# Order of the second conv's statistics and copy, aggregates by chunk, and first units in halves in a two-layer convolution kernel

## Chip, cores and metric

The kernel runs on one core of one Trainium2 chip. The metric is device time in microseconds (us) for one execution. TensorE is called PE here, VectorE DVE, ScalarE ACT, GpSimd POOL, and SyncE SP; SP issues nearly all DMAs. Each of these engines takes its instructions in order from a queue of its own.

## What is computed

The input is x, four images of 128 channels and 128 x 128 pixels, in fp32. Layer 0 is region attention (16 x 16 regions with a step of 14, four heads), merged back into an image `xf`, then a projection to 256 channels, a depthwise 5 x 5 convolution, a batch norm over all images, two Gelus, a projection back, and a residual. Layer 1 is two quantised 3 x 3 convolutions with batch norms. Cut to what matters here:

```python
y  = ln(xf) @ w_p0 + b_p0                  # 256 channels
ym = depthwise_5x5(y)
ym = batchnorm(ym)                         # mean and variance over images and pixels
y  = gelu(gelu(ym)) @ w_p2 + b_p2 + xf     # = x of layer 1, kept as identity

q   = round(clip(y, 0, 1) * 15)            # act_quant
c1  = conv3x3(q, quantised(w1))
q2  = round(clip(batchnorm(c1), 0, 1) * 15)
c2  = conv3x3(q2, quantised(w2))
out = batchnorm(c2) + identity
```

Each batch norm needs all of its input before the first output: three points at which all images must be through.

## The kernel before

Channels lie on the 128 partitions. The work has four stages.

**Attention and depthwise convolution** (to about 2316 us). Attention goes by bands of regions; the depthwise convolution runs beside it, and for its last unit (the last quarter of the last image) after it, in `conv_rest`. `conv_rest` goes through eight chunks k of 32 channels. Each `step(k)` does 256 and more small matmuls (L590), two ACT copies out of PSUM (L710), eight `bn_stats` on DVE (L714) and stores to DRAM (L719). The statistics lie in `st0`.

**Aggregation** (L1059 to L1079, then `affine`, L999 to L1005). 64 `bn_aggr` turn `st0` into `mvp` (one mean and variance for each of 64 groups); squares are added; the four channels that share a row are spread apart by products with `quad` (L1069, eight instructions into `ex`); four matmuls (L1071) sum over partitions; `affine` makes scale and shift for the Gelu. This part is not under a hand-written order: the planner places its instructions.

**Gelu stage** (`gelu_stage`). 64 units of 8 rows (U = 1024 pixels), 16 for each image. For each unit n: load `cv` (1 MB, L1185) and `xf` (512 KB, L1190) from DRAM, two Gelus (`gelus`: L1196 twice for the two channel halves with scale and shift, L1199 over both), the second projection (eight PE matmul instructions, L1208), bias and residual on DVE (L1216, writes y), clip on POOL (L1220), two quantising steps on DVE (L1226 and `to_int`, L1162) into the padded image `q1[b]`, and, two units behind, the first 3 x 3 convolution (`conv3x3`, 18 matmuls, L1150), its statistics (`stats_of`, L1158) and a copy out (`keep`, L1232). y is stored to `id_d` and the convolution to `c1_d`; the last image's convolution stays on chip in `c1_s`. The three buffers `cv` and `xfl` each are handed on from unit to unit.

**Last stages** (`last_stages`). A first pass over all 64 units: load `c1` (images 0 to 2 only, three buffers; for image 3 it is `c1_s`), relu with scale and shift on ACT (L1302), two quantising steps on DVE (L1303, L1162) into `q1[b]`, and behind it the second convolution with its statistics; for image 3, the 16 late units, ACT also copies the convolution out to `c1_s` (L1310). Then batch norm 2 (`rest2`) and a second pass, in which the convolution of images 0 to 2 is computed again and scaled (L1319), the identity added (L1320) and the result stored.

`most1` and `most2` aggregate the statistics of the first 120 of 128 half units ahead of time (L1025); `rest1` and `rest2` aggregate what is left and make scale and shift (L1034 to L1041).

The conv work, the Gelu stage and the last stages stand in `tc.manual_schedule(engines=MANUAL)`: PE, ACT, DVE and SP run in the order in which the code emits, POOL does not. So the order of the lines in the loop below is the order of each queue:

```python
for n in range(len(units) + 2):
    ...load_first(n + 2), load_id...
    if n < len(units):
        relu (ACT) of n; min/round (DVE) of n; to_int (DVE) of n
    if n >= 2:
        conv3x3 (PE) of n - 2; stats_of (DVE) of n - 2; copy (ACT) of n - 2 if image 3
```

PSUM tiles `pc` of the last stages have four buffers of two banks. A conv of unit n reads rows of units n-1, n and n+1 of `q1`.

Of the kernel before, what the change touches and what calls it, by code (L numbers as in the profile page):

```python
# [14 lines left out]
P = 128  # L15
# [31 lines left out]
def layers(  # L47
# [49 lines left out]
    c1_d = [dram.tile([P, P * P], F32, name=f"c1_d{b}") for b in range(B - 1)]  # L97
    id_d = [dram.tile([P, P * P], F32, name=f"id_d{b}") for b in range(B)]

    def vector(v, name):  # L100
        n = v.shape[0] // P
        t = const.tile([P, n], F32, name=name)
        nc.sync.dma_start(out=t, in_=v.rearrange("(h p) -> p h", p=P))
        return t

# [27 lines left out]
    with (  # L133
# [33 lines left out]
    units = [(b, 0, P // GR) for b in range(B - 1)] + [(B - 1, g, n) for g, n in ((0, 4), (4, 2), (6, 2))]  # L167

    sctx = ctx.enter_context(ExitStack())
    st0 = sctx.enter_context(tc.tile_pool(name=f"st0_{tag}", bufs=1)).tile(  # L170
        [P, NCK, 2, 4, len(units), 6], F32, name="st0"
    )


    with ExitStack() as actx:
# [492 lines left out]
        def conv_rest(n, w_t, u_t, c_t):  # L668

            b, g0, ng = units[n]
            early = 3
            at = GR + 2

            def load(k, a, z, g, m):
                for half in range(2):
                    ch = 32 * k + 16 * half
                    nc.sync.dma_start(
                        out=U[k][64 * half + 2 * a : 64 * half + 2 * z, g : g + m].rearrange(  # L680
                            "p g c x -> p g (c x)"
                        ),
                        in_=input_of(b, g0 + g, m, ch, 16, a, z),
                    )

            U = [u_t.tile([P, ng, 16, CW], F32, name=f"u{k}") for k in range(NCK)]
            W = [w_t.tile([P, 3, 16, 32], F32, name=f"w{k}") for k in range(NCK)]
            for k in range(NCK):
                weights(W[k], k, 0, 2, nc.gpsimd.dma_start)
            for k in range(early):  # L690
                load(k, 0, at, 0, 1)

            def late(k):
                if k < early:
                    load(k, 0, at, 1, 1)
                    load(k, at, GR + 4, 0, ng)
                else:
                    load(k, 0, GR, 0, ng)
                    load(k, GR, GR + 4, 0, ng)

            def step(k):
                sc = ps_s.tile([P, 2, 2, NT], F32, name=f"sc{k % 2}")
                pc = [
                    sc[:, half].rearrange("p a n -> p (a n)").rearrange("p (j g x) -> p j g x", j=4, g=ng)
                    for half in range(2)
                ]
                depthwise(pc, W[k], U[k], 16)
                for half in range(2):
                    cv = c_t.tile([P, 4, ng, CW], F32, name=f"c{half}")
                    nc.scalar.copy(  # L710
                        cv.rearrange("p j g x -> p (j g x)"), pc[half].rearrange("p j g x -> p (j g x)")
                    )
                    for j in range(4):
                        nc.vector.bn_stats(  # L714
                            st0[:, k, half, j, n, :], cv[:, j].rearrange("p g x -> p (g x)")
                        )
                    engine = (nc.sync, nc.scalar)[half]
                    for g in range(ng):
                        engine.dma_start(  # L719
                            out=bass.AP(  # L720
                                cv_d[b].tensor,
                                cv_d[b][g0 + g, 32 * k + 16 * half, 0:1].offset,
                                [[CW, P], [4 * GR * P, 4], [1, CW]],
                            ),
                            in_=cv[:, :, g],
                        )

            def run_all():
                for k in range(4):
                    late(k)  # L730
                for k in range(NCK):
                    step(k)
                    if k + 4 < NCK:
                        late(k + 4)

            return run_all
# [312 lines left out]

    mv0 = const.tile([P, 2, 2], F32, name="mv0")  # L1050
    with (
        tc.tile_pool(name=f"bn0_{tag}", bufs=1) as bn0,
        tc.tile_pool(name=f"ps_q_{tag}", bufs=1, space=PSUM) as ps_q,
    ):
        nk = NCK * 2 * 4
        mv = bn0.tile([P, 2, nk], F32, name="mvp")
        flat = st0.rearrange("p k a j n s -> p (k a j) (n s)")
        for k in range(nk):
            nc.vector.bn_aggr(mv[:, :, k], flat[:, k, :])  # L1059
        sq = bn0.tile([P, nk], F32, name="sqp")  # L1060
        nc.vector.tensor_tensor(sq, mv[:, 0, :], mv[:, 0, :], ALU.mult)
        nc.vector.tensor_tensor(mv[:, 1, :], mv[:, 1, :], sq, ALU.add)
        all1 = bn0.tile([P, 1], F32, name="all1")
        nc.vector.memset(all1, 1.0 / 32)
        pq = ps_q.tile([P, 2, 2], F32, name="pq")
        for m in range(2):
            ex = bn0.tile([P, nk, 4], F32, name=f"ex{m}")
            for q in range(4):
                nc.vector.tensor_scalar(ex[:, :, q], mv[:, m, :], quad[:, q : q + 1], None, ALU.mult)  # L1069
            for h in range(2):  # L1070
                nc.tensor.matmul(  # L1071
                    pq[:, m, h : h + 1],
                    ex.rearrange("p k q -> p (k q)")[:, h * P : (h + 1) * P], all1,
                    start=True, stop=True,
                )
        nc.vector.tensor_copy(mv0, pq)
        sq0 = bn0.tile([P, 2], F32, name="sq0")
        nc.vector.tensor_tensor(sq0, mv0[:, 0, :], mv0[:, 0, :], ALU.mult)
        nc.vector.tensor_tensor(mv0[:, 1, :], mv0[:, 1, :], sq0, ALU.subtract)  # L1079
    sc0, sh0 = affine(mv0[:, 0, :], mv0[:, 1, :], 2, bng, bnb, "0")  # L1080

    sctx.close()

# [56 lines left out]
    def rows_in(q, k):  # L1140
        return q[:, 1 + 2 * RB * k : 1 + 2 * RB * (k + 1), 1 : 1 + P]
# [14 lines left out]
    def stats_of(st, n, pc):  # L1156
        for h in range(2):
            nc.vector.bn_stats(st[:, 2 * n + h, :], pc[:, h])  # L1158

    def to_int(q, a):  # L1160

        nc.vector.tensor_scalar(  # L1162
            q, a.rearrange("p (r c) -> p r c", c=P), ROUND, None, ALU.subtract, saturate=False
        )
# [8 lines left out]
    def gelu_stage():  # L1173
        with (
# [7 lines left out]
            def load(n):  # L1182
                b, k = units[n]
                cv = ld.tile([P, 2, U], F32, name="cv")
                nc.sync.dma_start(  # L1185
                    out=cv,
                    in_=cv_d[b][k // 2].rearrange("(h p) n -> p h n", p=P)[:, :, pixels(k % 2)],
                )
                xf = ld.tile([P, U], F32, name="xfl")
                nc.sync.dma_start(out=xf, in_=xf_d[b][:, pixels(k)])  # L1190
                loaded[n] = cv, xf

            def gelus(n):
                cv = loaded[n][0]
                for h in range(2):
                    nc.scalar.activation(  # L1196
                        cv[:, h], cv[:, h], AF.Gelu, bias=sh0[:, h : h + 1], scale=sc0[:, h : h + 1]
                    )
                nc.scalar.activation(cv, cv, AF.Gelu)  # L1199

            def second_projection(n):
                b, k = units[n]
# [32 lines left out]

            for n in range(2):
                load(n)
            gelus(0)
            before1()
            before2()  # L1240
            for n in range(len(units) + 2):
                if n + 2 < len(units):
                    load(n + 2)
                while stores:
                    out_, in_ = stores.pop(0)
                    nc.sync.dma_start(out=out_, in_=in_)
# [17 lines left out]
    def last_stages():  # L1264
        with (
# [25 lines left out]
            for n in range(2):  # L1291
                load_first(n)
            sc1, sh1 = rest1()
            for n in range(len(units) + 2):
                if n + 2 < len(units):
                    load_first(n + 2)
                if n % 4 == 3 and n // 4 < 8:
                    load_id(n // 4)
                if n < len(units):
                    b, k = units[n]  # L1300
                    a = firsts.pop(n)
                    nc.scalar.activation(a, a, AF.Relu, bias=sh1, scale=sc1)  # L1302
                    nc.vector.tensor_scalar(a, a, 15.0, ROUND, ALU.min, ALU.add)  # L1303
                    to_int(rows_in(q1[b], k), a)
                if n >= 2:
                    b, k = units[n - 2]
                    pc = conv3x3(ps_d, n - 2, wq[1])
                    stats_of(st2, n - 2, pc)
                    if b == B - 1:
                        nc.scalar.copy(c1_s[:, pixels(k)], pc.rearrange("p h n -> p (h n)"))  # L1310
                if n == len(units) - 1:
                    most2()
            sc2, sh2 = rest2()
# [62 lines left out]
```

## Time and profile before

| | |
|---|---|
| median of three runs | 3279.0 us (3268.4, 3279.0, 3279.86) |
| profiled execution | 3272.91 us, of it the span 3271.1 us |
| granted PE clock, mean | 0.961 |
| PE busy in the span | 3100.5 us (95%) |
| DVE, ACT, POOL busy | 62%, 61%, 26% |
| end of depthwise convolution, first Gelu, first second-stage relu | 2315.6, 2324.7, 2808.1 us |
| start of the second pass's unbroken PE work, end of PE | 3068.9, 3261.2 us |
| DMA, mean | 208 GB/s; about 356 GB/s between 2356 and 2680 us |

A timeline row gives start and duration in us, engine, line, operation, output and input tiles, and in brackets the engine's idle time just before it with what ended that. A row of the chain of waits gives start, duration and what the end of the execution hung on then. A row "A <- B: s, n, m" of the waits says that A waited for B, s us in total, n times, m us at the longest. A matmul in fp32 shows as two records.

### The profile page before, as it was taken

What the parts mean: (1) busy time and instruction counts of PE and PEld (TensorE: products, weight loads), DVE (VectorE), ACT (ScalarE), POOL (GpSimd) and SP (SyncE); (2) the same over time, 40 slices, a digit from 0 to 9 for tenths busy, and PEclk for the clock granted to TensorE, in tenths of its full rate; (3) what the DMA queues carried; (4) which work ended last, traced back from release to release, by engine and by line L of the source; (5) the groups of instructions that cost most, each with busy time, mean ns of one, the idle gap of its engine ahead of it and who ended that gap; (6) DMA issues with size and microseconds to landing.
All of it is one profiled execution on the core that took longest, in us unless ns stands there. A gap on an engine that the chain in (4) does not pass through costs nothing.

```text
span 3271.1 us, 75716 instructions
## 1 busy us (share of the span) xinstructions
PE 3100.5 (95%) x30954; PEld 1550.6 (47%) x30954; DVE 2019.6 (62%) x3249; ACT 1990.9 (61%) x2654; POOL 837.5 (26%) x1058
## 2 busy tenths in 40 slices
PE   8999999999999999999999998886899999999998
PEld 4555554454444544444444445554444444444343
DVE  5877887766766667676655565442455555666543
ACT  5777776777776776777656564532467777333443
POOL 3444443333333333333322232211111111000000
PEclk9999999999999999999999998876799999999999
DMA  3555677888886788886899989857899999452398
GB/s 81 150 165 158 170 186 182 193 208 198 212 197 164 182 202 205 201 211 164 194 204 206 206 196 204 195 158 191 260 356 357 358 360 295 148 166 66 105 359 309
DMA packets 809827, 680.65 MB, mean 208 GB/s; under 512 B 580918, under 2 KB 695935, under 8 KB 809471
## 3 DMA queue, kind: packets, MB, share of 16 engines
q1 hardware_dynamic: 798879, 669.17, 75.6%
q8 instruction: 247, 4.05, 0.5%
q0 software_dynamic: 1024, 3.93, 0.5%
q10 hardware_dynamic: 9568, 2.61, 0.4%
q14 instruction: 109, 0.89, 0.1%
HBM read 408.72 MB, written 270.79 MB: 208 GB/s over the span
## 4 chain that ended last, share of the span: by engine, by line
PE 79%; DMA 7%; ACT 4%; issue 4%; DVE 3%; SPq 2%; POOL 0%; ACTq 0%; DVEq 0%; POOLq 0%
PE pc L1150 19%; PE pm L590 9%; PE sc L773 9%; PE po L836 8%; PE pb L1208 7%; PE pm L483 7%; PE pm L551 5%; PE pm L759 4%; PE po L844 4%; PE pm L367 3%; PE pm L535 3%; DMA y_d<-y 2%; ACT pt L781 1%; DMA u<-y_d 1%; DMA xn<-row 1%
## 5 line engine op out<-in xcount | busy, mean ns | idle before, releaser
L856 DVE RECIPROCAL rd<-po 128x256 f32<-128x256 f32 x324 | 569.2, 1757 | 462.1 <-PE po L844 459.3
L1150 PE MATMUL pc<-q,wq 128*128 128x512 fp8e4 x3168 | 702.1, 381 | 14.3 <-DVE q L1162 14.3
L781 ACT ACTIVATE pt<-sc 128x1024 f32<-128x1024 f32 x648 | 628.1, 1024 | 133.6 <-PE sc L773 69.1
L791 POOL TENSOR_TENSOR sm<-pt 128x512 f32<-128x512 f32 x324 | 413.1, 1275 | 1059.3 <-ACT pt L781 735.4
L1150 PEld LDWEIGHTS <-wq 128*128 128x128 fp8e4 x3168 | 309.1, 98 | 417.7 <-issue 50.3
L773 PE MATMUL sc<-q,kr 32*128 32x256 f32 x5184 | 404.6, 415 | 18.5 <-ACT pt L781 18.3
L590 PE MATMUL pm<-u,w 40*32 40x504 f32 (+5 forms) x7680 | 370.3, 506 | 32.7 <-DMA u<-y_d 21.0
L773 PEld LDWEIGHTS sc<-q,kr 32*128 32x128 f32 x5184 | 250.0, 191 | 258.6 <-issue 166.9
L836 PE MATMUL po<-pt,v 128*32 128x256 f32 x5184 | 361.2, 398 | 6.8 <-DVE part L860 5.5
L637 ACT COPY c<-pm 128x512 f32<-128x512 f32 (+1 forms) x256 | 132.4, 563 | 264.1 <-PE pm L590 243.4
L551 PE MATMUL pm<-xn,wp 128*128 128x512 f32 (+1 forms) x576 | 249.7, 564 | 36.4 <-ACT y L556 35.6
L556 ACT ACTIVATE y<-pm,bp 128x512 f32<-128x512 f32 (+1 forms) x288 | 183.0, 641 | 149.7 <-DMA y_d<-y 88.3
L791 DVE TENSOR_TENSOR sm<-pt 128x512 f32<-128x512 f32 x324 | 243.6, 752 | 25.7 <-ACT pt L781 25.7
L483 PE MATMUL pm<-xn,wqkv 128*128 128x512 f32 (+1 forms) x576 | 248.5, 560 | 2.7 <-ACT v L764 2.0
L590 PEld LDWEIGHTS pm<-u,w 40*32 40x32 f32 x7680 | 148.5, 113 | 213.1 <-issue 154.1
L641 DVE BATCH_NORM_STATS2 st<-c 128x6 f32<-128x512 f32 (+2 forms) x320 | 160.7, 550 | 132.2 <-ACT c L637 131.7
L1208 PE MATMUL pb<-cv,wp 128*128 128x512 f32 x512 | 232.9, 599 | 7.1 <-ACT cv L1199 7.1
L836 PEld LDWEIGHTS po<-pt,v 128*32 128x32 f32 x5184 | 139.7, 111 | 180.6 <-issue 105.6
L844 PE MATMUL po<-sm,ones 128*32 128x256 f32 x2592 | 206.3, 389 | 1.2 <-issue 1.2
L1158 DVE BATCH_NORM_STATS2 st<-pc 128x6 f32<-128x512 f32 x256 | 165.6, 689 | 67.5 <-PE pc L1150 67.5
L759 PE MATMUL pm<-wqkv,yr 128*128 128x128 f32 x1296 | 193.1, 290 | 1.3 <-ACT c L637 1.3
L759 PEld LDWEIGHTS pm<-wqkv,yr 128*128 128x128 f32 x1296 | 158.7, 191 | 69.9 <-issue 44.4
(157 smaller groups left out, 3445.4 us busy)
## 6 DMA issues: line engine op xcount, KB each, us to landing
cv<-cv_d SPq DMA_DIRECT2D x64, 1024.0 KB
u<-y_d SPq DMA_DIRECT2D x234, 256.0 KB
cv_d<-c SPq DMA_DIRECT2D x192, 256.0 KB
y_d<-y SPq DMA_DIRECT2D x160, 256.0 KB
xn<-row SPq DMA_DIRECT2D x76, 512.0 KB
xfl<-xf_d SPq DMA_DIRECT2D x64, 512.0 KB
id_d<-y SPq DMA_DIRECT2D x64, 512.0 KB
idt<-id_d SPq DMA_DIRECT2D x64, 512.0 KB
```

The source lines that it names most:

```text
L483: nc.tensor.matmul(pm[:, : n * P], wqkv[:, m * P : (m + 1) * P], held["xn"][hh], start=True, stop=True,)
L551: nc.tensor.matmul(pm[:, : n * P], wp0[:, h, :], held["xn"][hh], start=True, stop=True)
L590: nc.tensor.matmul(outs[half][32 * q : 32 * q + 32, j, :, a:z], wt[hs, s, c, :], ut[hs, :, c, a + s - 1 : z + s - 1], start=(s == 1), stop ...
L759: nc.tensor.matmul(pv[:, m, c, :], region(yr, j + m)[:, c * P : (c + 1) * P], wqkv[:, 2 * P :], start=True, stop=True,)
L773: nc.tensor.matmul(sc[h // 2][:, h % 2, kc, :].rearrange("p (r c) -> p r c", c=RS), region(kr, j)[hs, kc * P : (kc + 1) * P], queries(j, h ...
L781: nc.scalar.activation(pt, sc[p], AF.Exp)
L791: add(sm, pt[:, :, 0, :], pt[:, :, 1, :], ALU.add)
L836: nc.tensor.matmul(po[hs, 0, :], v[:, kc, hs], pt[h // 2][:, h % 2, kc, :], start=(kc == 0), stop=(kc == 1),)
L844: nc.tensor.matmul(po[hs, 1, :], ones, sm[h // 2][:, h % 2, :], start=True, stop=True)
L856: nc.vector.reciprocal(rd, po[:, 1, :])
L1150: nc.tensor.matmul(pc[:, h], w[:, t, :], q1[b][:, r + dy : r + dy + RB, dx : dx + P], start=(t == 0), stop=(t == 8),)
L1208: nc.tensor.matmul(pb[:, m], wp2[:, h, :], cv[:, h, px], start=(h == 0), stop=(h == 1))
```

## The change

It has five parts.

1. In the first pass of `last_stages` the convolution, its statistics and the copy come three units behind instead of two, and stand between the relu of unit n and its quantising steps.
2. There, and in `gelus`, unit 0 is taken in two halves of 512 pixels.
3. The depthwise `bn_aggr` are issued by `chunk_stats(k)`, eight after each `step(k)`, into a tile `mvp` that is allocated with `st0`; the rest of the aggregation, with `affine`, is put into the hand-written order; the eight products with `quad` become one instruction with repeated operands.
4. The first two loads of `cv` are issued ahead of the first two of `xf`.
5. The small per-channel vectors become slices of one tile of 24 columns.

```diff
+    vectors, used = const.tile([P, 24], F32, name="vectors"), [0]
     def vector(v, name):
         n = v.shape[0] // P
-        t = const.tile([P, n], F32, name=name)
+        t = vectors[:, used[0] : used[0] + n]
+        used[0] += n
...
+    mvp = stp.tile([P, 2, NCK * 2 * 4], F32, name="mvp")
+    def chunk_stats(k):
+        flat = st0[:, k].rearrange("p a j n s -> p (a j) (n s)")
+        for m in range(8):
+            nc.vector.bn_aggr(mvp[:, :, 8 * k + m], flat[:, m, :])
...
                 for k in range(NCK):
                     step(k)
+                    chunk_stats(k)
                     if k + 4 < NCK:
                         late(k + 4)
...
     with (
+        nullcontext() if safe else tc.manual_schedule(engines=MANUAL),
...
-        for k in range(nk):
-            nc.vector.bn_aggr(mv[:, :, k], flat[:, k, :])
+        mv = mvp
...
+        ex = bn0.tile([P, 2, nk, 4], F32, name="ex")
+        mq = [mv.rearrange("p m k -> p (m k)"), ex.rearrange("p m k q -> p (m k) q")]
+        nc.vector.tensor_tensor(
+            mq[1],
+            bass.AP(mq[0].tensor, mq[0].offset, [*mq[0].ap, [0, 4]]),
+            bass.AP(quad.tensor, quad.offset, [quad.ap[0], [0, 2 * nk], quad.ap[1]]),
+            ALU.mult,
+        )
         for m in range(2):
-            ex = bn0.tile([P, nk, 4], F32, name=f"ex{m}")
-            for q in range(4):
-                nc.vector.tensor_scalar(ex[:, :, q], mv[:, m, :], quad[:, q : q + 1], None, ALU.mult)
             for h in range(2):
                 nc.tensor.matmul(
                     pq[:, m, h : h + 1],
-                    ex.rearrange("p k q -> p (k q)")[:, h * P : (h + 1) * P], all1,
+                    ex[:, m].rearrange("p k q -> p (k q)")[:, h * P : (h + 1) * P], all1,
...
-    sc0, sh0 = affine(mv0[:, 0, :], mv0[:, 1, :], 2, bng, bnb, "0")
+        sc0, sh0 = affine(mv0[:, 0, :], mv0[:, 1, :], 2, bng, bnb, "0")
...
             def gelus(n):
-                cv = loaded[n][0]
-                for h in range(2):
-                    nc.scalar.activation(
-                        cv[:, h], cv[:, h], AF.Gelu, bias=sh0[:, h : h + 1], scale=sc0[:, h : h + 1]
-                    )
-                nc.scalar.activation(cv, cv, AF.Gelu)
+                for px in (slice(0, U // 2), slice(U // 2, U)) if n == 0 else (slice(0, U),):
+                    cv = loaded[n][0][:, :, px]
+                    for h in range(2):
+                        nc.scalar.activation(
+                            cv[:, h], cv[:, h], AF.Gelu, bias=sh0[:, h : h + 1], scale=sc0[:, h : h + 1]
+                        )
+                    nc.scalar.activation(cv, cv, AF.Gelu)
...
             for n in range(2):
                 load(n)
+            for n in range(2):
+                load_xf(n)
...
                 if n + 2 < len(units):
                     load(n + 2)
+                    load_xf(n + 2)
...
-            for n in range(len(units) + 2):
+            for n in range(len(units) + 3):
...
                 if n < len(units):
-                    b, k = units[n]
                     a = firsts.pop(n)
-                    nc.scalar.activation(a, a, AF.Relu, bias=sh1, scale=sc1)
-                    nc.vector.tensor_scalar(a, a, 15.0, ROUND, ALU.min, ALU.add)
-                    to_int(rows_in(q1[b], k), a)
-                if n >= 2:
-                    b, k = units[n - 2]
-                    pc = conv3x3(ps_d, n - 2, wq[1])
-                    stats_of(st2, n - 2, pc)
+                    parts = (slice(0, RB), slice(RB, 2 * RB)) if n == 0 else (slice(0, 2 * RB),)
+                    for h in parts:
+                        px = slice(h.start * P, h.stop * P)
+                        nc.scalar.activation(a[:, px], a[:, px], AF.Relu, bias=sh1, scale=sc1)
+                if n >= 3:
+                    b, k = units[n - 3]
+                    pc = conv3x3(ps_d, n - 3, wq[1])
+                    stats_of(st2, n - 3, pc)
                     if b == B - 1:
                         nc.scalar.copy(c1_s[:, pixels(k)], pc.rearrange("p h n -> p (h n)"))
+                if n < len(units):
+                    b, k = units[n]
+                    for h in parts:
+                        px = slice(h.start * P, h.stop * P)
+                        nc.vector.tensor_scalar(a[:, px], a[:, px], 15.0, ROUND, ALU.min, ALU.add)
+                        to_int(rows_in(q1[b], k)[:, h], a[:, px])
                 if n == len(units) - 1:
                     most2()
```

More of the change, by code (lines that the diff above doesn't have):

```diff
@@ L169, in layers @@
     sctx = ctx.enter_context(ExitStack())
-    st0 = sctx.enter_context(tc.tile_pool(name=f"st0_{tag}", bufs=1)).tile(
-        [P, NCK, 2, 4, len(units), 6], F32, name="st0"
-    )
+    stp = sctx.enter_context(tc.tile_pool(name=f"st0_{tag}", bufs=1))
+    st0 = stp.tile([P, NCK, 2, 4, len(units), 6], F32, name="st0")
+    mvp = stp.tile([P, 2, NCK * 2 * 4], F32, name="mvp")
[3 more added lines that the diff above has]
+            nc.vector.bn_aggr(mvp[:, :, 8 * k + m], flat[:, m, :])
     with ExitStack() as actx:
@@ L1055, in layers @@
         nk = NCK * 2 * 4
-        mv = bn0.tile([P, 2, nk], F32, name="mvp")
-        flat = st0.rearrange("p k a j n s -> p (k a j) (n s)")
-        for k in range(nk):
-            nc.vector.bn_aggr(mv[:, :, k], flat[:, k, :])
+        mv = mvp
         sq = bn0.tile([P, nk], F32, name="sqp")
@@ L1188, in load, with load_xf @@
                 )
+                loaded[n] = [cv]
+            def load_xf(n):
+                b, k = units[n]
                 xf = ld.tile([P, U], F32, name="xfl")
                 nc.sync.dma_start(out=xf, in_=xf_d[b][:, pixels(k)])
-                loaded[n] = cv, xf
+                loaded[n].append(xf)
             def gelus(n):
-                cv = loaded[n][0]
-                for h in range(2):
-                    nc.scalar.activation(
-                        cv[:, h], cv[:, h], AF.Gelu, bias=sh0[:, h : h + 1], scale=sc0[:, h : h + 1]
-                    )
-                nc.scalar.activation(cv, cv, AF.Gelu)
+                for px in (slice(0, U // 2), slice(U // 2, U)) if n == 0 else (slice(0, U),):
[5 more added lines that the diff above has]
+                    nc.scalar.activation(cv, cv, AF.Gelu)
             def second_projection(n):
@@ L1299, in last_stages @@
                 if n < len(units):
-                    b, k = units[n]
                     a = firsts.pop(n)
-                    nc.scalar.activation(a, a, AF.Relu, bias=sh1, scale=sc1)
-                    nc.vector.tensor_scalar(a, a, 15.0, ROUND, ALU.min, ALU.add)
-                    to_int(rows_in(q1[b], k), a)
-                if n >= 2:
-                    b, k = units[n - 2]
-                    pc = conv3x3(ps_d, n - 2, wq[1])
-                    stats_of(st2, n - 2, pc)
+                    parts = (slice(0, RB), slice(RB, 2 * RB)) if n == 0 else (slice(0, 2 * RB),)
[6 more added lines that the diff above has]
+                    stats_of(st2, n - 3, pc)
                     if b == B - 1:
                         nc.scalar.copy(c1_s[:, pixels(k)], pc.rearrange("p h n -> p (h n)"))
+                if n < len(units):
+                    b, k = units[n]
+                    for h in parts:
+                        px = slice(h.start * P, h.stop * P)
+                        nc.vector.tensor_scalar(a[:, px], a[:, px], 15.0, ROUND, ALU.min, ALU.add)
+                        to_int(rows_in(q1[b], k)[:, h], a[:, px])
                 if n == len(units) - 1:
```

## The prediction

> **What bounds the kernel now.** I read the page's engine table and 40 slices first: PE is busy 95% of the span, so only places where PE waits are worth anything. Then the waits by stretch, for the idle that the change can reach.
>
> ```profile
> PE 3100.5 (95%) x30954; PEld 1550.6 (47%) x30954; DVE 2019.6 (62%) x3249; ACT 1990.9 (61%) x2654; POOL 837.5 (26%) x1058
> ```
>
> ```profile
> PE pc L1150 <- DVE q L1162: 8.3, 10, 0.8
> ```
>
> The second line is from the waits between 3000 and 3072 us: ten times PE waited for a quantise, 8.3 us in all. These are the 16 late units of the last image. The chain of waits shows the loop that paces them, one turn from statistics to statistics:
>
> ```profile
> 3010.10 1.21 DVE st L1158 x2
> ...
> 3011.39 1.01 ACT c_s L1310
> 3012.40 1.15 ACT c_s L1302
> ...
> 3013.57 0.70 DVE c_s L1303
> ...
> 3014.30 0.70 DVE q L1162
> 3015.00 1.21 DVE st L1158 x2
> ```
>
> A turn is 3015.00 - 3010.10 = 4.90 us: DVE statistics of unit n-2, ACT copy of n-2, ACT relu of n+1 (queued behind that copy on ACT), DVE's two quantising steps of n+1, then the next statistics (queued behind those on DVE). PE needs only 18 matmuls, 3.91 us (the chain's "3.91 PE pc L1150 x18" pieces). So the two in-order queues pass one token to and fro, and PE has a hole in each turn.
>
> Two starts are the other holes. The timeline at the first Gelu unit (start, duration):
>
> ```profile
> 2324.71 2.37 ACT L1196 ACTIVATE cv<-cv,shift,scale 128x1024 f32<-128x1024 f32 x2 [1.74 <-DVE shift L1005]
> 2327.12 1.91 ACT L1199 ACTIVATE cv<-cv 128x2048 f32<-128x2048 f32 x1
> 2329.08 13.49 PE L1208 MATMUL pb<-cv,wp 128*128 128x512 f32 x24 [4.77 <-ACT cv L1199]
> ```
>
> PE waits for the whole of unit 0. And at the first late unit (first relu at 2808.07):
>
> ```profile
> 2809.35 0.69 DVE L1303 TENSOR_SCALAR c1l<-c1l 128x1024 f32<-128x1024 f32 x1 [1.36 <-ACT c1l L1302]
> 2810.08 0.70 DVE L1162 TENSOR_SCALAR q<-c1l 128x1024 fp8e4<-128x1024 f32 x1
> 2810.83 39.50 PE L1150 MATMUL pc<-q,wq 128*128 128x512 fp8e4 x169 [6.02 <-DVE q L1162]
> ```
>
> PE starts 0.05 us after the quantise of unit 0, before unit 1 is quantised: dependencies go by regions of a tile.
>
> [...] So the copy must wait for the statistics of the same unit; the trace agrees (copy at 3011.39, statistics ended 3011.31), and no reordering removes that wait, only what queues behind it. [...] the first eight matmuls of L1208 take 6.63 us in the chain, later eights 3.43; after the 6.02 us idle at 2804.8 thirteen conv matmuls take 0.43 us each, later ones 0.217.
>
> **Part 1, the late units.** Relu(n+1) now stands before copy(n-2) on ACT, and on DVE the statistics of n-3 stand before the quantising of n. No instruction is added. Say conv(n-3) ends at T. Statistics of n-3: T+1.2; ACT copy: T+2.3; relu(n+1): T+3.5. DVE goes from T+1.2 to the quantise of n, whose relu ran in the turn before: T+2.6. PE runs conv(n-2) until T+3.9, then conv(n-1), which reads up to the first row of unit n: ready 1.3 us before. DVE has 1.21+1.40 = 2.6 us a turn, ACT 1.01+1.15 = 2.2, both under 3.91: PE is the pace. What it saves: conv(48) ends at 3005.06; PE resumes after its last hole at 3068.92 with 3 matmuls of conv(62) left (0.65), so conv(62) ends at 3069.57. Unhindered it ends at 3005.06 + 14 x 3.906 = 3059.74. Difference **9.8 us** (8.3 of counted idle, the rest matmuls that the trace shows longer [...]). Behind it PE streams to the end (the chain's "192.21 PE pc L1150 x885"), so an earlier start moves the end one for one, if the last pass holds its pace: it moved 321 GB/s in that stretch against 356 in the Gelu stage, so DMA has room. The aggregate of the early units (L1025, 3.38 us on DVE) now follows the quantise of unit 63 with statistics of 61 to 63 behind it; the last statistics come after conv(63) anyway, and PE has three more convs and four PSUM buffers as cover: 0. Bounds: 0 to 9.8.
>
> In the 48 earlier units DVE's order in time is what it was (quantise n, statistics n-2, quantise n+1 reads the same shifted by one), ACT has no copy, and SP issues the same loads: 0. The load of n+2 waits for the quantise of n-1 on SP, as before. Cover: see the slower rival.
>
> **Part 2, first late unit in halves.** Relu of 512 instead of 1024: L1302 takes 1.24 us; [...] DVE's steps take 0.69 and 0.70 for 1024 elements, 0.29 for 256 (L377), so about 0.42 each. [...] **1.0 us** saved. Conv(0) needs row 4, the second half, from its seventh matmul; six cold ones last 2.6 us and that half is ready 0.9 us after the first. Three small instructions are added, on queues with slack here. Bounds: 0 to 2 [...].
>
> **Part 3, first Gelu unit in halves.** [...] PE starts 1.74 earlier. The whole unit ends 0.8 us later [...], and with it Gelus 1 and 2 on ACT; the first product's end, and not ACT, decides next. The chain goes "6.63 PE pb L1208 x8", then "7.06 DMA cv<-cv_d" (load 3 waits for unit 0's buffer), then Gelu 3: that load is issued 1.7 us earlier and so is y(0)'s store, on which y(2) and the copy before Gelu 4 wait. Working it through: product 2 comes 0.7 earlier, products 3 and 4 1.7. From 2356 on PE has no hole (323.6 busy of 323.6), so **1.7 us** is kept. Bounds: [...] 0.8 lost if PE had to wait for both halves.
>
> **Part 4, depthwise statistics.** The 64 aggregates by chunk already run after each chunk's statistics in this trace (eight in 1.53 us from 2298.13, and so on, with PE at work until 2315.5): 0. Only the tail from 2319.39 is new:
>
> ```profile
> L1071 PE MATMUL pq<-all,ex 128*128 128x1 f32 x8 | 1.8, 351 | 5.0 <-DVE ex L1069 5.0
> ...
> L1069 DVE TENSOR_SCALAR ex<-mvp,quad 128x64 f32<-128x64 f32 x8 | 1.5, 277 | 0.0
> ```
>
> Eight steps (1.5 us, half beside the first matmuls) become one of 512 elements. [...] It waits for the squares, and all matmuls wait for it: start 2320.75, end 2322.6, against 2322.41. The written order keeps some 0.1 us of foreign DVE work out of the chain: net **+0.1**. Bounds -0.5 to +1.5 (the foreign work, about 2.5 us on DVE, put in front). The vectors in one tile, and the load of xf after both cv: same DMAs on SP; first cv landed at 2321.65, table load ended 2322.97, Gelu began 2324.71, so 1.7 us of cover; xf is first read at 2335.74. 0.
>
> **Sum**: -9.8 - 1.0 - 1.7 + 0.1 = **-12.4 us**. The profiled execution took 3272.9 (span 3271.1), so 3260.5 (span 3258.7) in its terms. It lies below the median of the runs shown, 3279.0; they scatter from 3268.4 to 3279.9. I take the middle of 3272.9 and 3279.0 as base: 3276 - 12.4 = **3264**.
>
> **Rivals.** (a) *Only the late units pay*: PE waits for whole unit 0 at both starts (a region reckoned as one block). -9.8 + 0.8 + 0.1 = -8.9: 3267. Against it: PE's start 0.05 us after quantise 0. Chance 0.13. (b) *The order does not break the loop*, because something else queues on ACT or the last pass cannot take the earlier start: only 2.6 remains, 3273. For it: copy still waits for statistics; against it: the sums 2.6 and 2.2 under 3.91. Chance 0.07. (c) *Slower*: the loop through the load buffers. In the 48 units a buffer goes load, relu, quantise, load; quantise waits behind statistics, which wait for PE.
>
> ```profile
> 2839.74 1.24 ACT L1302 ACTIVATE c1l<-c1l,shift,scale 128x1024 f32<-128x1024 f32 x1 [2.75 <-DMA c1l<-c_d]
> 2841.04 1.29 DVE L1158 BATCH_NORM_STATS2 st<-pc 128x6 f32<-128x512 f32 x2 [1.29 <-PE pc L1150]
> 2842.25 0.68 DVE L1303 TENSOR_SCALAR c1l<-c1l 128x1024 f32<-128x1024 f32 x1
> ```
>
> Relu ends at 2840.98, quantise starts 2842.25: 1.27 us of slack in a turn of three units (11.7). If the new order sets it back by d, each unit loses (d-1.27)/3, 48 units 16(d-1.27); beyond d = 2.05 the 12.4 are gone; at 2.6, 3285. Against it: quantise already follows the statistics. Chance 0.05.
>
> **Numbers.** Forecast 0.75. 0.5% (16 us) is about what a measurement of this kernel can tell from no change; 12.4 is 0.38%, so the forecast itself is mostly "same": of its 0.75 about 0.27 passes the bound [...]. Slower: (c) and scatter, 0.06. Range: low 3253 (forecast with 3 us more and the fast execution's 8 below base), high 3274 (rival b).
>
> **Right or wrong.** Right: late turns of 3.9 us, no PE wait for quantise between 3000 and 3060; relu before copy on ACT; PE 1.8 us after the first late relu and 2.6 after the first Gelu; the last pass as long as before. Wrong: turns still near 4.9, PE holes in the last pass or in the Gelu stage, or relus landing later than statistics.

## The result and the profile after

The changed kernel takes 3267.95 us (median of 19 runs, 3258.45 to 3278.22) against 3274.57 of the kernel before beside it (19 runs, 3260.93 to 3284.77): ratio 0.9978, 95% interval 0.9968 to 0.9989, so 7.2 us less (3.6 to 10.5). The profiled execution took 3264.2 us with a span of 3262.4; before it was 3272.91, so 8.7 less in the two traces.

First the page's engine table again:

```profile
PE 3089.8 (95%) x30954; PEld 1544.8 (47%) x30954; DVE 2018.7 (62%) x3244; ACT 1991.5 (61%) x2658; POOL 837.6 (26%) x1058
```

Its shares are the same, and tell nothing of where the time went. The timeline of a late turn does (start, duration, engine, line):

```profile
3010.43 1.29 DVE L1172 BATCH_NORM_STATS2 st<-pc 128x6 f32<-128x512 f32 x2 [1.28 <-PE pc L1164]
3011.65 0.68 DVE L1340 TENSOR_SCALAR c_s<-c_s 128x1024 f32<-128x1024 f32 x1
3011.82 1.01 ACT L1335 COPY c_s<-pc 128x1024 f32<-128x1024 f32 x1 [1.73 <-DVE st L1172]
3012.36 0.70 DVE L1176 TENSOR_SCALAR q<-c_s 128x1024 fp8e4<-128x1024 f32 x1
3012.73 1.24 ACT L1328 ACTIVATE c_s<-c_s,shift,scale 128x1024 f32<-128x1024 f32 x1
3014.34 1.29 DVE L1172 BATCH_NORM_STATS2 st<-pc 128x6 f32<-128x512 f32 x2 [1.28 <-PE pc L1164]
```

A turn is now 3014.34 - 3010.43 = 3.91 us, the 18 matmuls' own time. The quantise (L1340) starts as the statistics end (3011.65, and 3010.43 + 1.29 = 3011.72), before the relu below it (L1328): it reads the relu of the turn before. DVE now waits 1.28 us for PE in each turn. The waits between 3000 and 3072 us have no row any more in which PE waits for a quantise. In the chain of waits the whole of the first pass and the second is one piece (start, duration):

```profile
2813.62 438.95 PE pc L1164 x2016
```

Before, the same 2016 matmuls took from 2810.83 to 3261.13, 450.3 us, so it is 11.3 less now. PE's last piece in the chain of before is this one:

```profile
3068.92 192.21 PE pc L1150 x885
```

Now the two starts, in the timeline, the first Gelu unit and then the first late unit:

```profile
2330.91 1.52 ACT L1216 ACTIVATE cv<-cv,shift,scale 128x512 f32<-128x512 f32 x2 [1.92 <-DVE shift L1016]
2332.46 1.06 ACT L1219 ACTIVATE cv<-cv 128x1024 f32<-128x1024 f32 x1
...
2333.57 6.11 PE L1228 MATMUL pb<-cv,wp 128*128 128x512 f32 x8 [3.06 <-ACT cv L1219]
...
2340.28 3.70 PE L1228 MATMUL pb<-cv,wp 128*128 128x512 f32 x8 [0.60 <-ACT cv L1219]
...
2811.83 3.78 ACT L1328 ACTIVATE c1l<-c1l,shift,scale 128x512 f32<-128x512 f32 x4 [0.83 <-DVE shift L1052]
2812.68 0.43 DVE L1340 TENSOR_SCALAR c1l<-c1l 128x512 f32<-128x512 f32 x1 [0.93 <-ACT c1l L1328]
2813.14 0.43 DVE L1176 TENSOR_SCALAR q<-c1l 128x512 fp8e4<-128x512 f32 x1
...
2813.62 16.66 PE L1164 MATMUL pc<-q,wq 128*128 128x512 fp8e4 x70 [5.06 <-DVE q L1176]
```

PE starts 2.66 us after the first Gelu (4.37 before) and 1.79 us after the first relu (2.76 before): the regions of the halves are told apart. But look at the first column: the first Gelu starts at 2330.91, before it was 2324.71. That is 6.2 us **later**. The new aggregation doesn't account for it. First the last aggregates of before and ACT's load of the Gelu's table, then the same and the tail of the aggregation in the changed kernel:

```profile
2317.82 1.53 DVE L1059 BATCH_NORM_AGGREGATE mvp<-st 128x2 f32<-128x36 f32 x8
...
2321.69 1.28 ACT L1196 ACT_TABLE_LOAD   x1 [4.97 <-DMA cv<-cv_d]
```

```profile
2324.77 0.61 DVE L181 BATCH_NORM_AGGREGATE mvp<-st 128x2 f32<-128x36 f32 x3
...
2325.93 0.69 DVE L1077 TENSOR_TENSOR ex<-mvp,quad 128x512 f32<-128x512 f32 x1
...
2326.77 1.84 PE L1085 MATMUL pq<-all,ex 128*128 128x1 f32 x8 [5.20 <-DVE ex L1077]
...
2327.71 1.28 ACT L1216 ACT_TABLE_LOAD   x1 [4.97 <-DMA cv<-cv_d]
```

From the end of the depthwise aggregates to the first Gelu it is 5.53 us, 5.36 before. The other 6.0 us were lost by 2325.4, in the attention and depthwise stage. There ACT, DVE, POOL and SP have the same instructions in the same order in both traces, but for one small memset on DVE (128x1) that comes 100 us later, and for part 4's loads at the very end. How far the changed kernel is behind there wanders: 4.3 us ahead at 1178 us, 1 to 3 behind at 1600, 10 behind at 2085, 6 behind at the end. The table load is the mark between the stages in what follows. So the account of the two traces is -14.7 us from it to the end, +6.0 before it: -8.7.

### The profile page after: what moved, and what is told of

Same layout as the page of the kernel before. It is cut to its first block, busy times and chain, and to the rows that moved or that the text cites. A ratio compares the mean times of both kernels' runs of the same rounds, so it can differ in the third digit from the quotient of the medians.

```text
span 3262.4 us, 75716 instructions
## 1 busy us (share of the span) xinstructions
PE 3089.8 (95%) x30954; PEld 1544.8 (47%) x30954; DVE 2018.7 (62%) x3244; ACT 1991.5 (61%) x2658; POOL 837.6 (26%) x1058
## 3 DMA queue, kind: packets, MB, share of 16 engines
q0 software_dynamic: 1024, 3.93, 0.4%
## 4 chain that ended last, share of the span: by engine, by line
PE 80%; DMA 7%; issue 4%; ACT 4%; SPq 3%; DVE 3%; POOL 0%; ACTq 0%; DVEq 0%; POOLq 0%
PE pc L1164 21%; PE pm L600 9%; PE sc L784 9%; PE po L847 8%; PE pm L493 7%; PE pb L1228 7%; PE pm L561 5%; PE pm L770 4%; PE po L855 4%; DMA y_d<-y 3%; PE pm L377 3%; PE pm L545 3%; ACT pt L792 2%; DVE rd L867 1%; DMA u<-y_d 1%
## 5 line engine op out<-in xcount | busy, mean ns | idle before, releaser
L792 ACT ACTIVATE pt<-sc 128x1024 f32<-128x1024 f32 x648 | 628.0, 1024 | 128.2 <-PE sc L784 62.6
L566 ACT ACTIVATE y<-pm,vectors 128x512 f32<-128x512 f32 (+1 forms) x288 | 182.9, 641 | 152.4 <-DMA y_d<-y 98.3
```

Source lines behind the costliest of these rows:

```text
L792: nc.scalar.activation(pt, sc[p], AF.Exp)
```

## The experiments

The ratios are against runs of the kernel before on the same chip as the experiment, 27 to 29 in each set; its median was 3263.3, 3259.3 and 3259.5 us on the three chips, so times of different sets are not compared. In each short diff "-" is what the kernel before (or the one after, where it says so) has; "..." stands for lines left out, and where a run takes the whole unit as its only part, the plain lines are shown. Parts 1, 2 and the storage of parts 3 and 5 have runs of their own. Part 4 has none, and the new tail of the aggregation only one together with the storage.

**The late order alone.** Kernel before, with the order of part 1 and no halves, old aggregation and vectors:

```diff
                     nc.scalar.activation(a, a, AF.Relu, bias=sh1, scale=sc1)
-                    nc.vector.tensor_scalar(a, a, 15.0, ROUND, ALU.min, ALU.add)
-                    to_int(rows_in(q1[b], k), a)
-                if n >= 2:
+                if n >= 3:
...
+                if n < len(units):
+                    b, k = units[n]
+                    nc.vector.tensor_scalar(a, a, 15.0, ROUND, ALU.min, ALU.add)
+                    to_int(rows_in(q1[b], k), a)
```

> The kernel before with part 1 alone (three units behind, statistics and copy ahead of the quantising steps); no halves, no chunk aggregates, small vectors in tiles of their own. Theory A (the 12 to 15 us that the changed kernel's trace gains after the first Gelu are real, and some 6 us are lost in the attention stage because the tiles of parts 3 and 5 lie at other addresses): here no address changes in the attention stage, so the whole 9.8 us of the late units show: ratio 0.997. Theory B (no stage is lost; the attention stage only scatters, and the late units bring less in a usual execution): ratio about 0.998 to 0.999. In the profile both: late turns of 3.91 us, no wait of PE for a quantise between 3000 and 3060 us.

Ratio 0.9970 (0.9959 to 0.9981), -9.8 us (-6.2 to -13.4); its PE goes through the 2016 matmuls in 439.88 us. The term of part 1 holds by itself.

**The old storage in the changed kernel.** Kernel after, with parts 3 and 5 undone (aggregation and vectors as before):

```diff
-        t = vectors[:, used[0] : used[0] + n]
+        t = const.tile([P, n], F32, name=name)
...
-                    chunk_stats(k)
```

> The changed kernel with parts 3 and 5 undone: aggregation and small vectors as before (own tiles, planner's order), late order, halves and load order as changed. Theory A: the attention stage is back at its old pace, the rest keeps its gain: 0.9955 to 0.9962 (12.4 to 15 us), clearly below the changed kernel run beside it. Theory B: the same as the changed kernel, about 0.998.

0.9951 (0.9938 to 0.9964), -16.0 us, more than the whole change gives.

**The new storage alone.** Kernel before, with the vectors in one tile and `mvp` allocated beside `st0`; no instruction is moved:

```diff
+    vectors, used = const.tile([P, 24], F32, name="vectors"), [0]
...
-        t = const.tile([P, n], F32, name=name)
+        t = vectors[:, used[0] : used[0] + n]
...
+    mvp = stp.tile([P, 2, NCK * 2 * 4], F32, name="mvp")
```

> The kernel before with the small vectors as slices of one tile and the tile of the aggregates allocated beside st0; every instruction and every queue's order as before. Theory A: slower by about 6 us, ratio 1.002. Theory B: 1.000 within the interval.

1.0017 (1.0008 to 1.0025), 5.5 us slower. From the table load to the end it takes 948.8 us, as before (949.4); the loss lies in front of it.

**The changed kernel beside these.**

> The changed kernel itself, unedited, to stand beside the other three on one chip. Both theories: about 0.998 against the kernel before. In its profile from the first Gelu to the end 931.5 us as in the trace at hand[...].

0.9967 (0.9954 to 0.9980), -10.8 us; the interval overlaps with the first one. Its profile takes 932.7 us from the first Gelu to the end, as expected. The gap to the kernel with the old storage is again some 5 us.

So where tiles lie costs time. The new storage saves a few small tiles, and all that is allocated behind them moves. In the built programs the tiles that the attention stage's DMAs write or read fall into two groups by where they start, modulo 256 bytes in the partition. The first group is `u` and `c` (input and output of the depthwise convolution), `xt` (rows of x) and `w` (depthwise weights); the second is `y2`, `xn`, `xf` and `xr`. The two start at 128 and 192 in the kernel before, at 64 and 128 in the one after. Tiles that only the engines use move with them. The next five kernels move them, by an unused tile (a spacer), by shifting small constants, or by both; no instruction is added.

**After, moved to the old places.**

```diff
     mvp = stp.tile([P, 2, NCK * 2 * 4], F32, name="mvp")
+    stp.tile([P, 16], F32, name="spacer")
```

> The changed kernel with a spacer of 64 bytes a partition behind the tile of the aggregates, nothing else. The attention stage's tiles then start at the same places within 256 bytes as in the kernel before (the depthwise input u at 128, as before; 64 in the changed kernel). Theory C (the 5 to 6 us of the attention stage are the tiles' start addresses alone): the loss is gone, 0.995 as in the run with the old layout; 1 KB packets back to a median of 64 ns. Theory D (it is the slices of one tile, or the aggregates' tile itself): no change, 0.9967.

0.9956 (0.9939 to 0.9972), -14.3 us: with 64 unused bytes the changed kernel comes to what it gives with the old storage (0.9951). The interval alone doesn't set it apart from the changed kernel without the spacer (0.9954 to 0.9980).

**Before, moved to the new places.**

```diff
     st0 = stp.tile([P, NCK, 2, 4, len(units), 6], F32, name="st0")
+    stp.tile([P, 48], F32, name="spacer")
```

> The kernel before with a spacer of 192 bytes a partition behind st0, nothing else: the attention stage's tiles start where the changed kernel has them (u at 64 within 256). Theory C: slower as the layout alone was, 1.0017; 1 KB packets at a median of 68 ns. Theory D: 1.000.

1.0016 (1.0006 to 1.0026), +5.2 us, with an unused tile only. The same loss as with the new storage, and the interval leaves out 1, so it is the place and not the one tile.

**After, moved to 0 and 64.** `eps_t` and `mhalf` become slices of `vectors`:

```diff
-    eps_t = const.tile([P, 1], F32, name="eps_t")
+    eps_t = vectors[:, 20:21]
...
-    mhalf = const.tile([P, 2], F32, name="mhalf")
+    mhalf = vectors[:, 21:23]
```

> The changed kernel with the two constant tiles eps_t and mhalf moved into the vectors' tile: 64 bytes less, so that u and the depthwise output c start at a multiple of 256 bytes (xn and y2 at 64). Theory C, in the form that a multiple of 256 is what a transfer wants: at least as fast as the 64-byte spacer, 0.994 to 0.995, 1 KB packets under 64 ns. Theory C in a form where other tiles count (xn, y2): between. Theory D: 0.9967.

0.9930 (0.9912 to 0.9948), -22.8 us. The page's DMA queue row (packets, MB, share of 16 engines' time), of the kernel with the old places first and of this one second:

```profile
q1 hardware_dynamic: 798879, 669.17, 74.8%
```

```profile
q1 hardware_dynamic: 798879, 669.17, 72.8%
```

The same packets and bytes, and less time in them. In the trace the median packet of 1 KB (81,097 of them before the first Gelu, those of `u` among them) takes 47 ns with `u` at 0, 65 at 128.

**Before, moved to 0 and 64.**

```diff
+    stp.tile([P, 32], F32, name="spacer")
```

> The kernel before with a spacer of 128 bytes a partition behind st0: u, c, x's rows and the depthwise weights start at a multiple of 256 bytes, nothing else changes. Theory C (start addresses of transfers): 1 KB packets at a median of 47 ns instead of 64, and the attention stage 8 to 9 us shorter (the step from 64 bytes to 0 was 12 us, from 128 to 64 it cost 5.5): ratio 0.997. If the gain of the kernel with u at 0 came from the moved constants: 1.000.

0.9982 (0.9973 to 0.9991), -5.9 us: the sign without any other edit, the size smaller than expected. The 1 KB packets take 51 ns.

**After, with all of them at 0.** As for 0 and 64, and `qb` and `quad` too, with a spacer between the two groups of tiles:

```diff
+        small.tile([P, 16], F32, name="spacer2", bufs=1)
```

> The changed kernel with four small constants in the vectors' tile and 64 bytes behind the pool of small tiles, so that every tile of the attention stage that a DMA reads or writes (x rows, u, c, w, y2, xn, xf) starts at a multiple of 256 bytes. If y2, xn and xf count too: below the 0.993 of the kernel with u and c alone, 0.991 to 0.992. If only u and c count: 0.993.

0.9904 (0.9886 to 0.9922), -31.3 us. It is the fastest here and beats both kernels. Some 17 us of it (9 to 25, from the two intervals) are storage alone: the same order and halves at the old places gave -14.3 on another chip.

The start of the table load ahead of the first Gelu, in one profiled execution of each, puts these together. The first pair is the two traces above, and a set is the experiments that ran on one chip:

| places | first pair | first set | second set | third set |
|---|---|---|---|---|
| 64 and 128 | 2327.7 | 2322.9, 2320.2 | 2317.9 | |
| 128 and 192 | 2321.7 | 2312.7, 2313.3 | 2308.3, 2310.4 | 2311.1, 2314.0 |
| 0 and 64 | | | 2301.9 | 2306.7 |
| 0 and 0 | | | | 2292.1 |

In each column the order is the same. One execution alone would show little, since those of one kernel lie up to 23 us apart (3249.8 to 3272.9 in the second set). Behind that point no place matters: 934.7 and 936.0 us to the end in the two profiles of the changed kernel, 934.8 with it at the old places, 934.4 at 0 and 64, 934.1 at 0 and 0.

**The order with two units of lag.** Is the third unit needed? Kernel before, with convolution, statistics and copy of n-2 set between relu and quantise:

```diff
                     nc.scalar.activation(a, a, AF.Relu, bias=sh1, scale=sc1)
-                    nc.vector.tensor_scalar(a, a, 15.0, ROUND, ALU.min, ALU.add)
-                    to_int(rows_in(q1[b], k), a)
                 if n >= 2:
...
+                if n < len(units):
+                    b, k = units[n]
+                    nc.vector.tensor_scalar(a, a, 15.0, ROUND, ALU.min, ALU.add)
+                    to_int(rows_in(q1[b], k), a)
```

> The kernel before with statistics and copy put between relu and quantising steps, but still two units behind: the position without the third unit of lag. If the position breaks the loop (relu no longer behind the copy, statistics no longer behind the quantising steps): late turns of 3.91 us, PE without a wait for a quantise, as with three units. If the lag is needed (the convolution of n-1 reads the first row of unit n, quantised 2.6 us after the end of n-2): PE waits up to 0.5 us a turn, turns of 3.9 to 4.4 us, or the whole first pass slows.

One execution, 3250.0 us. The timeline of a late turn:

```profile
3007.75 1.29 DVE L1158 BATCH_NORM_STATS2 st<-pc 128x6 f32<-128x512 f32 x2 [1.28 <-PE pc L1150]
3008.96 0.68 DVE L1317 TENSOR_SCALAR c_s<-c_s 128x1024 f32<-128x1024 f32 x1
3009.13 1.01 ACT L1312 COPY c_s<-pc 128x1024 f32<-128x1024 f32 x1 [1.75 <-DVE st L1158]
...
3011.66 1.30 DVE L1158 BATCH_NORM_STATS2 st<-pc 128x6 f32<-128x512 f32 x2 [1.28 <-PE pc L1150]
```

3.91 us a turn, no wait of PE for a quantise between 3000 and 3072, and the 2016 matmuls in 440.01 us: as with three behind.

**The lag alone.** Kernel before, three behind, at the old position behind the quantise:

```diff
-                if n >= 2:
+                if n >= 3:
```

> The kernel before with three units of lag but the old position: relu, quantising steps, then convolution, statistics and copy of n-3. If the position makes the gain (as two units behind suggested): the loop is whole, relu(n+1) behind the copy on ACT and the statistics behind the quantising steps on DVE, so late turns of 4.90 us and 8 us of PE waiting for quantises, as before; total from the first Gelu to the end unchanged, 946 us. If the lag makes it: turns of 3.91 us.

One execution, 3257.37 us. A late turn, in the timeline, and PE's waits between 3000 and 3072 (us in total, times, longest):

```profile
3009.02 1.29 DVE L1158 BATCH_NORM_STATS2 st<-pc 128x6 f32<-128x512 f32 x2
3010.39 1.01 ACT L1310 COPY c_s<-pc 128x1024 f32<-128x1024 f32 x1 [2.75 <-DVE st L1158]
3011.30 1.24 ACT L1302 ACTIVATE c_s<-c_s,shift,scale 128x1024 f32<-128x1024 f32 x1
3012.58 0.69 DVE L1303 TENSOR_SCALAR c_s<-c_s 128x1024 f32<-128x1024 f32 x1 [2.27 <-ACT c_s L1302]
...
3013.91 1.29 DVE L1158 BATCH_NORM_STATS2 st<-pc 128x6 f32<-128x512 f32 x2
```

```profile
PE pc L1150 <- DVE q L1162: 4.2, 5, 0.8
```

The turn is still 3013.91 - 3009.02 = 4.89 us: copy, relu, quantise, statistics, one after the other. Unlike what was expected, PE waits only five times instead of ten, since it sets out one unit (3.91 us) further behind the quantise, and each turn uses up 0.98 us of that. First pass and second take 445.6 us, 4.7 less than before. The lag buys lead once; the position breaks the loop.

**The halves alone.** Kernel before with part 2:

```diff
+                for px in (slice(0, U // 2), slice(U // 2, U)) if n == 0 else (slice(0, U),):
...
+                    parts = (slice(0, RB), slice(RB, 2 * RB)) if n == 0 else (slice(0, 2 * RB),)
```

> The kernel before with unit 0 in halves at both starts, nothing else. If the halves' gains add up as in the prediction: PE 2.65 us after the first Gelu (4.37 before) and 1.8 us after the first late relu (2.76), from the first Gelu to the end 946.4 - 2.7 = 943.7 us[...]; late turns still 4.90 us. If the second half's wait eats the start: 946.

One execution, 3261.05 us. PE starts 2.66 us after the first Gelu and 1.80 after the first late relu; the late waits are the old ones (8.3 us, ten times). From table load to end it takes 945.2 us, 4.2 less than before, and 3.1 to 3.9 less than the kernels before with their tiles at other places (948.3 to 949.1).

## Why the prediction was right, and where not

The time forecast, 3264, was 4 us under the measured 3268, and inside the range. That closeness is in part luck: a loss of 5.5 us that it did not have was partly hidden by some 1 us more gain than forecast and by a base of 3276, 1.4 us above the measured 3274.6. The forecast sum of -12.4 was too large: measured are -7.2 (-3.6 to -10.5).

- **Late units, -9.8: right**, with its mechanism. The kernel that has it alone measured -9.8 (-6.2 to -13.4), with turns of 3.91 us and no hole. That the copy waits for the statistics is still seen (it starts at 3011.82, the statistics end at 3011.72), as in three other orders (3011.39 and 3011.31 in the kernel before, 3009.13 and 3009.04 with the position alone, 3010.39 and 3010.31 with the lag alone); what makes it wait, no trace shows. Only nothing hangs on that wait now. What the prediction did not see is that the position alone does this, with the old lag of two.
- **First late unit in halves, -1.0: right for the start, a part of the rest is chance.** PE started 0.97 us earlier; each DVE step took 0.43 us, 0.42 was estimated. On top comes the clock. In the two traces above it was granted at 0.50 for 6.8 us in the kernel before (2809.4 to 2816.3) and for 3.4 us in the changed kernel (2812.9 to 2816.3), and at 1.00 behind that. In the seven traces without halves PE's matmuls were slow (0.43 us, later ones 0.217) until 10.6 to 12.0 us after PE fell idle. In the seven with halves they were so until 7.6 to 8.0 us in four, and until 10.2 to 11.0 in three. The changed kernel itself has both: 6 slow matmuls in its first profile, 14 in its second. The two groups lie some 3 us apart, about what the two traces above differ by in the time at 0.50 (3.4 us); what sets that time was not shown. On average 9.4 matmuls were slow instead of 13.0, some 0.8 us more saved, so -1.8 in all; one execution need not show it. The bound "0 to 2" holds it; the value taken was its middle.
- **First Gelu unit in halves, -1.7: nearly right.** PE's start, 1.71 us earlier against 1.74, is right. What half an activation takes, on which this start and the late one rest, was the author's estimate; in the changed kernel's trace two of 512 elements take 1.52 us and one of 1024 takes 1.06, in the trace of before 2.37 and 1.91 for the whole unit. The Gelus of unit 0 take 5.11 us in all against 4.32, so the whole unit does end 0.8 later. From the first Gelu to the end of the stage's last convolution the seven traces with halves take 476.7 to 478.1 us, the seven without 478.6 to 480.1: 2.0 less on average, 2.4 in the first pair. One step of the working was wrong, though: "the first product's end, and not ACT, decides next". The second product waits 0.60 us for ACT (its row at 2340.28), and it ends 13.1 us after the first Gelu in all seven, whether the first product took 5.1 or 6.5 us. Where the last 0.3 us come from stays open.
- **Aggregation tail, +0.1: right** (+0.17). The one product of 512 elements takes 0.69 us; the forecast rested there on an estimate of the author's.
- **"The vectors in one tile ... same DMAs on SP ... 0": wrong.** This is the term that failed. The DMAs are the same in number, bytes and order; what the sentence passed over is that the tiles they write into lie elsewhere. It measured +5.5 us (2.6 to 8.2) alone, and +5.2 (2.0 to 8.5) with a spacer alone. In 16 of the first stage's 28 slices the page of before has the DMA engines busy for eight tenths or more, so what a packet costs was to be asked there.

With these the terms add up: -9.8 - 1.8 - 2.0 + 0.2 + 5.5 = -7.9, against -7.2 timed and -8.7 in the profiled pair. Without the last term it would be -13.4; the changed kernel at the old places measured -14.3 (-9.1 to -19.9). Of the rivals, (a) predicted 3267, closer in number to the measured time, but its mechanism is refuted: both starts were earlier. (b) and (c) did not come about: the loop is broken, and the 48 earlier units run unbroken in the chain.

**Not settled** is why 64 and 128 is worse than 128 and 192, nor is it shown why places count at all. The packets set only 0 apart: the median packet of 1 KB takes 47 and 46 ns in the changed kernels at 0, 51 in the kernel before at 0, against 64 to 71 at 64 and at 128. Between 64 and 128 they do differ a little, 68 to 71 ns against 64 to 66, yet the share of DMA time was no higher at 64 (74.4% in the kernel before moved to the new places, 74.8% in the one after moved to the old). Nor do packets explain the second group's move to 0: from 0 and 64 to 0 and 0 the 1 KB packets went from 47 to 46 ns only and the share of DMA time rose (72.8% to 73.3%), yet the kernel got faster (0.9930 to 0.9904, though these intervals overlap). DVE's and ACT's busy time in that stage is the same within 0.6% at all places that were compared. Which transfer or access pays there was not isolated, nor that the DMAs alone pay.

## What to carry to other kernels

When in-order queues pass one token round, look for the instruction that can stand behind the wait with its input a turn old; here where a unit stands in the turn decided (3.91 us a turn with two units of lag and with three, 4.89 with the lag alone), and more lag only delayed the holes (five waits instead of ten). An edit that adds no instruction can still move every tile behind it (5.5 us lost here): where DMA engines are busy most of the time, as in 16 of the first stage's 28 slices here, look up where the destination tiles start, and try them at multiples of 256 bytes, which gave -31.3 us here against -14.3 at the old places. When a sum fits the total roughly, still check each stage: here a gain of 14.7 us and a loss of 6.0 stood behind one small number.

## What was not expected of the hardware

Where tiles start within 256 bytes of a partition changes the time of this kernel's first stage: in the third set of profiles the table load came at 2292.1 us with all at 0, at 2311.1 and 2314.0 with the old places. In whole times the kernel before is at 1.0016 with its tiles at 64 and 128 and at 0.9982 with them at 0 and 64; the changed kernel is at 0.9967 as it is, at 0.9956 with the old places and at 0.9904 with all at 0. The Gelu stage's loads of 1 MB did not show it: `cv` started at 0, 192 and 128 in the changed kernels as it is, at 0 and 64, and at 0 and 0, and from the table load to the end they took 934.7 and 936.0, 934.4 and 934.1 us.
